# Four tiles of a gather move from ScalarE's row DMAs to GpSimd, in a graph layer on one core

## The chip, the cores and the metric

The kernel runs on one core of a Trainium2 chip. Five engines work side by side and meet at semaphores: TensorE (PE, with its weight loads PEld), VectorE (DVE), ScalarE (ACT), GpSimd (POOL) and SyncE (SP). SP, ACT and POOL each have a queue from which DMAs are issued. The metric is the device time of one execution in microseconds; lower is better. A profiled execution has its own time, and a span, which is the time from its first to its last instruction.

## The reference

A message-passing layer over 12,500 nodes of 128 features and 400,000 edges, sorted by destination, with a residual and a normalisation of rows:

```python
rbf = jnp.exp(-(distances[:, None] - centers) ** 2 / (2.0 * width * width))
cut = 0.5 * (jnp.cos(jnp.pi * distances / CUTOFF) + 1.0) * (distances <= CUTOFF)
W = (jax.nn.silu(rbf @ fw1 + fb1) @ fw2 + fb2) * cut[:, None]
messages = (h[src] @ pw + pb) * W
agg = jax.ops.segment_sum(messages, dst, num_segments=num_atoms)
y = h + (jax.nn.silu(agg @ mw1 + mb1) @ mw2 + mb2)
out = _layernorm(x + y)
```

The edge lengths are such that most edges lie beyond the cutoff and add nothing. h[src] is the gather: for every edge that counts, one row of 128 float32 (0.5 KB) from a table of nodes.

## The kernel before

**Stages.** First the table proj = x @ pw + pb is computed for all nodes, 4 x 128 rows at a time, and stored to DRAM. Beside it VectorE packs the edges: seven chunks (0 to 6) of the edge list are compacted to those within the cutoff by shifts under masks (copies under a predicate at L539, passes over the listing at L545 and L549), written to a list in DRAM by GpSimd (L524), read back and unpacked to indices, places and cutoffs. Packing goes on while the main loop runs, a few steps between one quad and the next.

**Quads.** Packed edges are taken in 139 quads (q = 0 to 138) of QT = 4 tiles of 128 edges (j = 0 to 3). For each quad: `basis` makes the radial functions on ScalarE (L1150, L1154), `first` and `silu` the first layer on TensorE and ScalarE for two quads at once (L1166, L1172), `second` the second layer into a bank of PSUM (L1184). `message` (L1200) multiplies it on VectorE with the gathered rows. `place` (L1213) makes on VectorE a 0/1 matrix, times the cutoff, of the destinations; `sum_up` (L1234) multiplies messages and matrix on TensorE into sums of a window of nodes, and `add` (L1268) adds these on VectorE to aggT. Nodes whose edges are all done go through the second network and the normalisation in between (L1282 and on). The last quad, 138, is multiplied tile by tile (L1200, four products of 128 columns).

**Who fetches the rows.** A tile's 128 rows are usually fetched by one indirect DMA of GpSimd (`fetch`, L1098) into a buffer of the quad: 13 buffers named quad and, up to quad 62, 8 more named x. The first 12 quads gather from the input x, the others from proj. In 13 quads (`SINGLY`) tile j = 0 is left out by `fetch` and comes in 128 single DMAs of one row, each with its address in a register (`one_row`, L1074), into buffers of their own (row_sb). Nine of the quads (`BY_SP`) are fetched from SP's queue, four (`BY_ACT`: 36, 68, 100, 134) from ScalarE's. ScalarE's single DMAs are put by `beside` behind its instructions in `basis` and `silu`, three, two or four at a time (`HIDE`), as long as its list of rows lasts. In such a quad `message` first waits for a semaphore that counts the rows, multiplies tile 0 alone (L1197), and then the other three tiles (L1200).

**What sets the order.** All engines' orders are written out by hand in the program; it keeps a clock of its own (`clock` for VectorE, `pool` for GpSimd, which grows by 1.29 for each gather) to decide which piece of packing to put where. A gather gets its place in two steps: `fetches` puts it on a queue when the program's clock says so, and `gathers` issues it when VectorE's program has as many instructions as the table `PACE` asks for that quad and tile (`pace` interpolates between the table's pairs of quad and count). `vectors` is the list of VectorE's instructions of some kinds, and the issued gather is tied to the one at the count: it waits on the chip until that instruction is done.

Of the kernel before, what the change touches and what calls it, by code (L numbers as in the profile page):

```python
# [57 lines left out]
DIRECT = 32  # L58
FIRST = 16
LISTS = 5  # L60
PACE = ((2, 17), (3, 26), (4, 36), (5, 54), (7, 95), (9, 125), (10, 144), (12, 170), (18, 250), (24, 324), (30, 373), (36, 458), (42, 544), (48, 612), (54, 691), (60, 754), (66, 826), (72, 902), (78, 982), (84, 1071), (90, 1139), (96, 1218), (102, 1306), (108, 1357), (114, 1414), (120, 1461), (126, 1518), (132, 1580), (138, 1646), (139, 1666))
VECTORS = ("TensorScalarPtr", "TensorTensor", "CopyPredicated", "TensorReduce", "TensorCopy",
           "BNStats")
SPILL = 4
# [6 lines left out]
PACK_US = 1.5  # L71
EARLY_US = 7
BY_SP = (22, 45, 62, 67, 86, 102, 113, 124, 135)
BY_ACT = (36, 68, 100, 134)
SINGLY = tuple(sorted(BY_SP + BY_ACT))
A_ROW = 0.58
A_ROW_LATE = 0.42
# [15 lines left out]
def kernel(  # L93
# [347 lines left out]
    vectors, queue = [], []  # L441
# [8 lines left out]
    def pace(q, j):  # L450

        (a, u), (b, v) = next((k for k in zip(PACE, PACE[1:]) if q < k[1][0]))
        return int(u + (v - u) * (q + j / QT - a) / (b - a))

    def gathers(must=0):

        while queue and (queue[0][0] < must or len(vectors) >= pace(*queue[0])):
            q, j = queue.pop(0)
            fetch(q, js=(j,))
# [372 lines left out]
    def unpack(c):  # L832
# [34 lines left out]
        def paired(dt, name):  # L867
            if c == 0:
                k = OWN_0[name]
                if k > 3:  # L870
                    return aggT[:np_, N - (k - 3) * 256:N - (k - 4) * 256].bitcast(dt)
                v = quad_sb[GOT - 1] if k < 2 else own(1, "msg", 0)
                v = v.rearrange("p j f -> p (j f)").bitcast(dt)
                return v[:np_, k % 2 * 256:k % 2 * 256 + 256]
            return work.tile([64, 256], dt, name=name, bufs=1)[:np_]
# [69 lines left out]
        if mine:  # L945
            at_row = work.tile([64, P], I32, name="at_row", bufs=3)
            nc.vector.tensor_scalar(at_row[:np_], f_src[:, :P], float(4 * H), None, op0=OP.mult)
            for q in mine:
                p = 2 * (q - QB[c])
                singles[q in BY_ACT].extend((q, e, at_row[p:p + 1]) for e in range(P))  # L950
        part = paired(I32, "part")
# [82 lines left out]
    def own(q, name, also):  # L1034

        k = q % (4 if q >= OWN_4 else 2)
        if k > 1:
            return quad_sb[OTHERS[2 * also + k - 2]]
        if (name, k) not in own_sb:
            own_sb[name, k] = keep.tile([P, QT, H], F32, name=f"{name}{k}")  # L1040
        return own_sb[name, k]
# [20 lines left out]
    def one_row(act):  # L1062

        eng, of, n = (nc.scalar, BY_ACT, ACT_AT_ONCE) if act else (nc.sync, BY_SP, AT_ONCE)
        q, e, i = singles[act].pop(0)
# [26 lines left out]
    def fetch(q, idx=None, table=None, js=range(QT)):  # L1092
        got = quad_sb[place_of(q) if q >= 0 else 0]
        for j in js:
            if q in SINGLY and j == 0:
# [4 lines left out]
                in_offset=bass.IndirectOffsetOnAxis(ap=i, axis=0))  # L1100
            if PACE[0][0] <= q < NL:
                tc.add_manual_dep(
# [85 lines left out]
    def message(q, js=(0, QT)):  # L1188
        gathers(q + 1)
        msg = own(q, "msg", 0)  # L1190
        a, b = js
        if q in SINGLY and a == 0:
            act = q in BY_ACT
            k = (BY_ACT if act else BY_SP).index(q)
            assert q in alone and all(s[0] != q for s in singles[act])
            nc.vector.wait_ge(row_sem[act][k % ROW_SEMS], 16 * P * (k // ROW_SEMS + 1))
            m = nc.vector.tensor_mul(msg[:, 0, :], pu_of[q][:, :H], alone.pop(q))  # L1197
            tc.declare_no_dep(m.ins, group="rows", reason="waits on row_sem")
            a = 1
        nc.vector.tensor_mul(msg[:, a:b, :], pu_of[q].rearrange("p (j f) -> p j f", j=QT)[:, a:b, :],  # L1200
                             got_of[q][:, a:b, :])
        if b == QT:
            free.append(pu_of.pop(q))
            got_of.pop(q)
        gathers()
        return msg
# [385 lines left out]
    for q in range(NL - 7):  # L1592
        while todo and q + 2 >= DIRECT // QT and todo[0] <= chunk_of(min(q + 2, NQ - 1)):
            go_on(todo[0])
        msg = message(q)
        nodes(q)
        most[0] = room(q)
# [71 lines left out]
    q = NL - 7  # L1669
    house(q)  # L1670
    msg = message(q)
    second(q + 2)
    sum_up(q, msg)
# [9 lines left out]
    q += 1  # L1683
    house(q)
    msg = message(q)
    second(q + 2)
    first(octs(q - 1))
# [206 lines left out]
```

## Time and profile before

| | |
|---|---|
| median of 3 runs | 715.56 us (713.54 to 716.36) |
| the profiled execution | 714.6 us, its span 713.1 us |
| mean granted TensorE clock | 0.927 |
| gathers (indirect DMAs of GpSimd into quad and x) | 48 from the input, 401 + 94 from proj |
| single-row DMAs | 1152 from SP, 512 from ScalarE, 0.5 KB each |
| moved by DMA | 91.45 MB, 128 GB/s on average |

Engines are PE, PEld, DVE, ACT, POOL and SP; an engine's name with a q (ACTq) is its sequencer, which issues DMAs and handles registers, and such instructions are not counted as busy. L1098 is line 1098 of the kernel. "out<-in" names what an instruction writes and reads. In a group, "x401" is a count, and three numbers with slashes are the shortest, median and longest duration in ns. Brackets give the idle time of the engine before an instruction and what ended it, inferred from semaphores; "issue" means that nothing in the profile was waited for. In a list of waits, "A <- B: 45.1, 21, 3.7" reads: A waited for B 45.1 us in total, 21 times, 3.7 at the longest. The chain of waits starts at the last instruction and follows back what released each step. The slices cut the span into 40 equal parts; a digit is the busy share in tenths.

### The profile page before, as it was taken

Reading aid. Unit: us, or ns where it says so; the run is one execution under the profiler, and the core shown is the slowest. Engines: PE = TensorE matmul, PEld = TensorE weight load, DVE = VectorE, ACT = ScalarE, POOL = GpSimd, SP = SyncE. Lnnn points to the kernel's source line nnn. Section 1 sums busy time; section 2 is a strip of 40 time slices with the busy share of each in tenths; the row PEclk is TensorE's granted clock in tenths of the full one; section 3 lists DMA queues with packets and bytes.
Section 4 is the critical chain, followed back from the end, with each engine's and each line's share of the span. In section 5 each row is a group of like instructions: output and inputs, shape, how many; then the busy total and the mean of one; then the engine's idle time right before and its main releaser. Section 6 shows DMA issues by size and latency. Waiting matters only on the chain.

```text
span 713.1 us, 15123 instructions
## 1 busy us (share of the span) xinstructions
PE 585.7 (82%) x3531; PEld 462.3 (65%) x3531; DVE 561.6 (79%) x1744; ACT 402.2 (56%) x568; POOL 528.5 (74%) x564
## 2 busy tenths in 40 slices
PE   6786767778988788798889997999788877798785
PEld 5775556556766576676677774777566655575673
DVE  8889899749999889989999995867554555475776
ACT  6547725144745667554665455668543843476455
POOL 6777777777777777777777777777777777777772
PEclk9999897799999899999988999999988999999998
DMA  8997443242434334342334344444442443334343
GB/s 255 338 290 227 149 127 105 61 136 84 112 102 134 85 87 116 100 131 85 98 104 116 107 136 110 142 115 142 120 123 72 128 130 97 101 102 142 92 126 105
DMA packets 54233, 91.45 MB, mean 128 GB/s; under 512 B 14384, under 2 KB 21776, under 8 KB 54138
## 3 DMA queue, kind: packets, MB, share of 16 engines
q0 software_dynamic: 17680, 36.44, 20.4%
q1 hardware_dynamic: 25172, 35.68, 15.2%
q10 hardware_dynamic: 11286, 18.31, 7.9%
q8 instruction: 29, 0.48, 0.3%
q14 instruction: 66, 0.54, 0.2%
HBM read 74.59 MB, written 15.79 MB: 127 GB/s over the span
## 4 chain that ended last, share of the span: by engine, by line
DVE 27%; DMA 15%; PE 14%; issue 8%; ACTq 4%; ACT 3%; DVEq 2%; POOL 2%; SPq 0%; POOLq 0%
DMA quad<-proj,srci 14%; DVE hot L1213 7%; PE ph L1166 4%; DVE msg L1200 4%; PE bank L1184 3%; DVE aggT L1268 3%; PE sums L1234 3%; ACTq L1074 2%; POOL quad L1098 2%; DVE quad L1213 2%; DVE bank L545 2%; DVE quad L1200 1%; DVEq L1243 1%; DVE r_d L539 1%; PE bank L1282 1%
## 5 line engine op out<-in xcount | busy, mean ns | idle before, releaser
L1098 POOL DMA_INDIRECT quad<-proj,srci x401 | 381.1, 950 | 122.4 <-issue 48.2
L1184 PEld LDWEIGHTS bank<-fw_sb,s 128*128 128x128 f32 x1112 | 160.1, 207 | 61.9 <-issue 51.6
L1184 PE MATMUL bank<-fw_sb,s 128*128 128x128 f32 x1112 | 160.5, 291 | 0.0
L1166 PE MATMUL ph<-rbf,w_sb 102*128 102x512 f32 x278 | 141.9, 635 | 13.0 <-ACT s L1172 9.5
L1234 PEld LDWEIGHTS sums<-hot,msg 128*128 128x128 f32 x816 | 108.9, 200 | 50.5 <-issue 22.8
L1172 ACT ACTIVATE s<-ph 128x1024 f32<-128x1024 f32 x70 | 71.3, 1018 | 116.9 <-PE ph L1166 116.5
L1213 DVE TENSOR_SCALAR hot<-iota_n,dl,cut 128x80 f32<-128x80 f32 (+4 forms) x408 | 109.1, 339 | 21.3 <-PE sums L1234 19.3
L1234 PE MATMUL sums<-hot,msg 128*128 128x80 f32 (+4 forms) x816 | 111.0, 281 | 12.9 <-DVE msg L1200 12.9
L1098 POOL DMA_INDIRECT x<-proj,srci x94 | 89.9, 957 | 29.2 <-issue 7.3
L1181 PE MATMUL bank<-fb_b,ones_b 96*128 96x512 bf16 x139 | 56.1, 403 | 44.2 <-DVE msg L1200 25.8
L1200 DVE TENSOR_TENSOR msg<-bank,quad 128x512 f32<-128x512 f32 (+1 forms) x78 | 52.3, 671 | 49.6 <-DMA quad<-proj,srci 45.1
L1166 PEld LDWEIGHTS ph<-rbf,w_sb 102*128 102x128 f32 x278 | 50.8, 203 | 52.4 <-issue 37.3
L1268 DVE TENSOR_TENSOR aggT<-aggT,sums 128x80 f32 (+4 forms) x209 | 53.9, 258 | 21.1 <-PE sums L1234 7.2
L1150 ACT ACTIVATE rbf<-d_sb,rbf_bias,rbf_scale 102x512 f32<-102x512 f32 x70 | 56.2, 803 | 7.8 <-issue 7.8
L1098 POOL DMA_INDIRECT quad<-in_x_dram,srci x48 | 47.5, 989 | 16.3 <-issue 5.5
L1172 ACT ACT_TABLE_LOAD x35 | 44.9, 1283 | 15.3 <-issue 14.9
L1154 ACT ACT_TABLE_LOAD x35 | 44.9, 1283 | 11.3 <-issue 9.4
L349 PEld LDWEIGHTS bank<-pw_sb,xT 128*128 128x128 f32 (+1 forms) x292 | 41.6, 207 | 13.3 <-ACT xT L1005 7.2
L1154 ACT ACTIVATE rbf<-rbf 102x512 f32<-102x512 f32 x70 | 44.1, 630 | 8.1 <-issue 5.7
L1234 PE MATMUL sums<-quad,quad 128*128 128x128 f32 (+3 forms) x296 | 42.8, 290 | 4.7 <-DVE quad L1200 4.6
L1200 DVE TENSOR_TENSOR quad<-bank,quad 128x512 f32<-128x512 f32 (+2 forms) x40 | 25.1, 628 | 26.9 <-DMA quad<-proj,srci 26.7
L1234 PEld LDWEIGHTS sums<-quad,quad 128*128 128x128 f32 x296 | 39.6, 206 | 6.9 <-DVE quad L1200 6.2
(281 smaller groups left out, 813.4 us busy)
## 6 DMA issues: line engine op xcount, KB each, us to landing
row_sb<-proj SPq DMA_DIRECT2D x1152, 0.5 KB
d_sb<-near_d ACTq DMA_DIRECT2D x67, 256.0 KB
x<-in_x_dram SPq DMA_DIRECT2D x46, 256.0 KB
row_sb<-proj ACTq DMA_DIRECT2D x512, 0.5 KB
quad<-proj,srci POOLq DMA_INDIRECT x401
proj<-hp SPq DMA_DIRECT2D x24, 256.0 KB
out_dram<-x SPq DMA_DIRECT2D x22, 256.0 KB
x<-proj,srci POOLq DMA_INDIRECT x94
```

Source lines behind the costliest of these rows:

```text
L349: nc.tensor.matmul(to[:m, k, :], lT[:, k * P:k * P + m], w, start=False, stop=(k == a + c - 1))
L1098: g = nc.gpsimd.indirect_dma_start(out=got[:, j, :], out_offset=None, in_=proj if table is None else table, in_offset=bass.IndirectOffsetO ...
L1150: a = nc.scalar.activation(rbf[:u], d[:u], AF.Square, bias=rbf_bias[:u], scale=rbf_scale[:u])
L1154: nc.scalar.activation(rbf[:u], rbf[:u], AF.Exp, scale=-1.0 / (2.0 * width * width))
L1166: nc.tensor.matmul(ph[:, h, :], w1_sb[:2 * KR, h, :], rbf[:2 * KR], start=True, stop=True)
L1172: nc.scalar.activation(s[:, :n], ph[:, :n], AF.Silu)
L1181: nc.tensor.matmul(pu, ones_b[:, :P], bias_b["fb2"].rearrange("k j f -> k (j f)"), start=True, stop=False)
L1184: nc.tensor.matmul(pu[:, j * H:(j + 1) * H], s[:, j * P:(j + 1) * P], fw2_sb, start=False, stop=(j == QT - 1))
L1200: nc.vector.tensor_mul(msg[:, a:b, :], pu_of[q].rearrange("p (j f) -> p j f", j=QT)[:, a:b, :], got_of[q][:, a:b, :])
L1213: nc.vector.tensor_scalar(hot[:, j, :wide(q)], iota_n[:, :wide(q)], dl[:, at[0], at[1]], cut[:, at[0], at[1]], op0=OP.is_equal, op1=OP.mult)
L1234: nc.tensor.matmul(pa[:, k * W:k * W + wide(q)], msg[:, j, :], hot[:, j, :wide(q)], start=(j % n == 0), stop=(j % n == n - 1))
L1268: nc.vector.tensor_add(to, to, pa[:, k * W:k * W + wide(q)])
```

## The change

ScalarE's list of quads becomes empty: tile 0 of quads 36, 68, 100 and 134 is gathered by GpSimd like any other tile, and these quads are multiplied in one product. SP keeps its nine. In the quads of SP, the product of tile 0 is taken off the list `vectors` at once, so that gathers are neither tied to it nor counted with it, and the counts in `PACE` are lower by as many from quad 42 on.

```diff
-PACE = ((2, 17), (3, 26), (4, 36), (5, 54), (7, 95), (9, 125), (10, 144), (12, 170), (18, 250), (24, 324), (30, 373), (36, 458), (42, 544), (48, 612), (54, 691), (60, 754), (66, 826), (72, 902), (78, 982), (84, 1071), (90, 1139), (96, 1218), (102, 1306), (108, 1357), (114, 1414), (120, 1461), (126, 1518), (132, 1580), (138, 1646), (139, 1666))
+PACE = ((2, 17), (3, 26), (4, 36), (5, 54), (7, 95), (9, 125), (10, 144), (12, 170), (18, 250), (24, 324), (30, 373), (36, 458), (42, 543), (48, 611), (54, 688), (60, 751), (66, 823), (72, 898), (78, 978), (84, 1065), (90, 1133), (96, 1211), (102, 1298), (108, 1349), (114, 1404), (120, 1452), (126, 1507), (132, 1569), (138, 1635), (139, 1653))
...
-BY_ACT = (36, 68, 100, 134)
+BY_ACT = ()
...
             m = nc.vector.tensor_mul(msg[:, 0, :], pu_of[q][:, :H], alone.pop(q))
+            vectors.pop()
             tc.declare_no_dep(m.ins, group="rows", reason="waits on row_sem")
```

## The prediction

> **What bounds the kernel now.** I began with the page's busy shares and slices, to see which engine never lets go:
>
> ```profile
> span 713.1 us, 15123 instructions
> ...
> PE 585.7 (82%) x3531; PEld 462.3 (65%) x3531; DVE 561.6 (79%) x1744; ACT 402.2 (56%) x568; POOL 528.5 (74%) x564
> ...
> DVE  8889899749999889989999995867554555475776
> ...
> POOL 6777777777777777777777777777777777777772
> ```
>
> By shares, PE leads and GpSimd is fourth. The slices say otherwise: VectorE is at nine tenths up to two thirds of the span and then falls to five, while GpSimd stands at seven in all slices but the first and last. An engine that is at one constant level below ten either gets its work at a constant rate, or has a constant gap after each instruction. The groups by line and the instructions in order of time decide (start, duration, engine, line, operation, in brackets the idle time before and what ended it):
>
> ```profile
> L1098 POOL DMA_INDIRECT quad<-proj,srci x401: 938/944/1188, 72.5 to 700.3; - x134
> L1098 POOL DMA_INDIRECT x<-proj,srci x94: 940/944/1097, 77.6 to 327.2; - x94
> ...
> L524 POOL DMA_INDIRECT packed<-line,at_i x7 | 7.3, 1043 | 2.7 <-issue 1.2 <-DVE base_i L661 0.9 <-DVE hot L1213 0.3
> ```
>
> ```profile
> 194.30 0.94 POOL L1098 DMA_INDIRECT x<-proj,srci  x1 [0.30 <-issue]
> 195.54 0.94 POOL L1098 DMA_INDIRECT x<-proj,srci  x1 [0.30 <-issue]
> ...
> 208.48 1.01 POOL L1098 DMA_INDIRECT x<-proj,srci  x1 [0.75 <-DVE hot L1213]
> ...
> 212.33 1.01 POOL L1098 DMA_INDIRECT x<-proj,srci  x1 [0.34 <-DVE hot L1213]
> ...
> 254.29 0.94 POOL L1098 DMA_INDIRECT quad<-proj,srci  x1 [0.39 <-DVE bank L545]
> ...
> 699.02 0.94 POOL L1098 DMA_INDIRECT quad<-proj,srci  x1 [0.30 <-issue]
> 700.27 0.94 POOL L1098 DMA_INDIRECT quad<-proj,srci  x1 [0.30 <-issue]
> ```
>
> A gather takes 0.944 us and the next starts 0.30 us later whatever is named as the releaser: a step of 1.25 us. From 72.5 to 700.3, 627.8 us, lie 401 + 94 = 495 gathers, which at 1.25 fill 618.8; the list writes in between (1.04 + 0.30 each, at most 7) take up to 9.4 more. The stream is full for 627.8 of 713.1 us. Only three gaps after 72.5 are over 0.31: 0.75, 0.34 and 0.39, together 0.45 + 0.04 + 0.09 = 0.6 us of real waiting, all for VectorE.
>
> The last question is whether the end hangs on the last gather. VectorE's products of the last quad:
>
> ```profile
> 699.98 0.27 DVE L1200 TENSOR_TENSOR quad<-bank,quad 128x128 f32<-128x128 f32 x1
> ...
> 701.13 0.28 DVE L1200 TENSOR_TENSOR quad<-bank,quad 128x128 f32<-128x128 f32 x1
> ...
> 702.43 0.28 DVE L1200 TENSOR_TENSOR quad<-bank,quad 128x128 f32<-128x128 f32 x1
> ...
> 703.29 0.29 DVE L1200 TENSOR_TENSOR quad<-bank,quad 128x128 f32<-128x128 f32 x1
> ```
>
> The quad is multiplied tile by tile as its four gathers land; the second and third products follow the gathers' step (1.15, 1.30 us), and the last starts 3.0 us after the last gather's start. So the end is that start plus 12.8 us (713.1 - 700.27). The kernel is a stream of gathers on one engine with a fixed tail.
>
> **The change, part by part.** First, what is taken from ScalarE:
>
> ```profile
> L1074 ACTq MOVE row_sb<-proj x512: 29/29/38, 145.3 to 640.6; - x171
> L1074 ACTq DMA_DIRECT2D row_sb<-proj x512: 227/228/543, 145.4 to 640.7; - x171
> L1197 DVE TENSOR_TENSOR msg<-bank,row_sb x8: 271/281/285, 202.4 to 635.2; 128x128 f32<-128x128 f32 x8
> L1197 DVE TENSOR_TENSOR quad<-bank,row_sb x5: 266/283/290, 375.0 to 690.1; 128x128 f32<-128x128 f32 x5
> ```
>
> 512 x (0.029 + 0.228) = 131.6 us of ScalarE's queue go, with the loads of the row addresses. That work sits in waits ScalarE has anyway, but not all of it:
>
> ```profile
> by line: DMA quad<-proj,srci 13.9%; issue 7.7%; DVE hot L1213 6.5%; PE ph L1166 4.5%; DVE msg L1200 3.8%; PE bank L1184 3.3%; DVE aggT L1268 2.8%; PE sums L1234 2.6%; ACTq L1074 2.3%; POOL quad L1098 1.8%; DVE quad L1213 1.8%; DVE bank L545
> ...
> ACT s L1172 <- PE ph L1166: 116.5, 46, 6.9
> ...
> DVE msg L1200 <- DMA quad<-proj,srci: 45.1, 21, 3.7
> ...
> DVE quad L1200 <- DMA quad<-proj,srci: 26.7, 15, 3.0
> ```
>
> The chain of waits puts 2.3%, 16.4 us, on ScalarE's row issues. I book this at nothing: the chain follows one path back, and beside it GpSimd went on without a gap. What ScalarE gains, PE and VectorE get earlier, and spend waiting for gathers, as VectorE already does for 45.1 + 26.7 us. Were GpSimd's stream not full, up to 16.4 us would come out (second rival).
>
> Second, VectorE. Of the 13 extra products of 0.28 us, four go; their quads' other product grows from 384 to 512 columns:
>
> ```profile
> 632.39 0.69 DVE L1200 TENSOR_TENSOR quad<-bank,quad 128x512 f32<-128x512 f32 x1 [2.88 <-DMA quad<-proj,srci]
> ...
> 635.76 0.56 DVE L1200 TENSOR_TENSOR msg<-bank,quad 128x384 f32<-128x384 f32 x1 [0.29 <-DMA quad<-proj,srci]
> ```
>
> That is 4 x (0.28 + 0.56 - 0.69) = 0.6 us less work, hidden in the same waits; the bound of cost is 0 to -0.6 us. These quads now wait for one more gather in place of a semaphore of rows; nothing else is queued behind that wait than before.
>
> Third, GpSimd gets four gathers of 128 rows, one each for quads 36, 68, 100 and 134, each just before its quad's other three. All later gathers, and the list writes after quad 36, are queued behind them. The bytes (512 rows of 0.5 KB) are the same and only change queues. A stretch without packing and one with VectorE nearly full give the same price (length, then busy time and count of PE, PEld, DVE, ACT, POOL, then clock, DMA share, GB/s):
>
> ```profile
> 200.00:320.00 120.00, 102.67 (x630) 82.02 (x629) 108.92 (x313) 72.49 (x88) 90.44 (x96) 0.93 0.37 106
> ...
> 480.00:701.00 221.00, 183.94 (x1080) 140.05 (x1078) 134.14 (x468) 127.81 (x187) 167.19 (x177) 0.95 0.40 113
> ```
>
> 120 / 96 = 1.25 and 221 / 177 = 1.249. Four make **+5.0 us**. Bounds: by the shortest, 4 x (0.938 + 0.30) = 4.95; by the longest, 4 x (1.188 + 0.30) = 5.95; I take the step, which most have.
>
> What lengthens a gather speaks on whether it is cheaper with ScalarE silent. The longest:
>
> ```profile
> 372.97 1.19 POOL L1098 DMA_INDIRECT quad<-proj,srci  x1 [0.31 <-DMA quad<-proj,srci]
> ...
> L1098 POOL DMA_INDIRECT quad<-proj,srci x401 | 381.1, 950 | 122.4 <-issue 48.2 <-DVE hot L1213 11.6 <-DVE aggT L1268 11.6
> L1098 POOL DMA_INDIRECT x<-proj,srci x94 | 89.9, 957 | 29.2 <-issue 7.3 <-DVE hot L1213 4.4 <-DMA x<-proj,srci 3.0
> ```
>
> Means of 950 and 957 against a median of 944 leave 401 x 6 + 94 x 13 = 3.6 us of lengthening in all; that is what could at most vanish. I take 0 of it: in 480 to 701, where ScalarE still issues rows, the mean is 167.19 / 177 = 0.945, so the rows lengthen nothing.
>
> The Trainium skill's page "SBUF — State Buffer", section "SBUF: two separate sides", has a rule against this change: a DMA that GpSimd issues needs descriptors written through a port pair that some VectorE instructions lock, while one issued by ScalarE does not. Its section "A bandwidth-pool intuition that's wrong (but worth ruling out)" gives 620 ns alone and some 3,100 ns beside a VectorE copy; by that factor of five, an estimate, four gathers would cost about 20 us. This trace shows nothing of that size, 1.19 us being its worst after 72.5.
>
> Fourth, the ties. A gather waits for a VectorE instruction that is counted in the list of names. The nine remaining row products leave the list and four cease to exist; the table's last entry falls by 13 (1666 to 1653), entries before quad 36 stay. So each gather stays tied to the same place in VectorE's work, give or take one instruction (0.3 us). As GpSimd comes 1.25 us later to each tie after quad 36, the three waits of 0.6 us in all should shrink. VectorE may be later too, since the program's own clock for GpSimd gains 1.29 us per added gather and may pull packing steps ahead (one listing pass: 0.69 us). Bounds -0.6 to +0.7; I take -0.4, the two late ones being short and the 0.75 being smaller than one added step.
>
> Sum: 5.0 - 0.4 = +4.6 us on a span of 713.1: 717.7. The profiled run took 714.6, 1.5 more than its span, and so 719.2; it lies 1.0 under the median of 715.56, so the median to expect is **720.2 us**, +0.64%.
>
> **Rivals.**
>
> 1. *The gathers get shorter (no change).* If rows and gathers do contend and all 3.6 us of lengthening and the 0.6 of waits go: 5.0 - 4.2 = +0.8, 716.4. For it: row fetches and gathers share the DMA engines. Against: the mean of 0.945 above.
> 2. *ScalarE's queue was the path (faster).* Its place is the stretch 145 to 641; the price is the 16.4 us of the chain, against 5.0 of gathers: 715.56 - 11.4 = 704.2. It decides as soon as GpSimd has idle time that VectorE or ScalarE causes; from 3.6 us of such time on, the result leaves "no change". The waits of 0.75 to 0.34 between 208 and 255 speak for it, their sum of 0.6 against it.
> 3. *The ties catch.* If VectorE's order shifts so that packing stands ahead of tied instructions where GpSimd is close behind (208 to 255), each of the two additions within the packing, quads 36 and 68, costs another 1.3 us: 5.0 + 2.6 = +7.6, 723.2. For it: the 0.39 behind a listing pass. Against: GpSimd is later too.
> 4. *Gathers starve beside VectorE.* If the freed ScalarE packs VectorE's work closer, so that all gathers after quad 36 (103 quads, some 400) come at the 957 ns of those into x, which run up to 327 us where VectorE is fullest, and not at 945: 400 x 0.012 = 4.8 on top of 4.6, 725.0. Against: VectorE's total work falls. It is the Trainium skill's rule above ("SBUF — State Buffer", "SBUF: two separate sides") at the size that the rows give.
>
> That the change does not do what it says can be ruled out from the code: with no quad for ScalarE, its list stays empty and the gathers are no longer skipped.
>
> **How the numbers follow.** Forecast 0.75, rivals 0.10, 0.05, 0.07, 0.03. The range is 717.8 (the sum less the shortened gathers' first 2 us and a low median) to 723.0 (the longest gathers and the tie's 0.7, or nearly all of rival 3). A measurement of this kernel tells about 0.5%, 3.6 us, from no change. Faster: rival 2, 0.05. Same: rival 1, and 0.04 from the forecast's low edge, 0.14. Slower: 0.81.
>
> **What would show it.** Gathers in the changed profile: 404 + 95 (quad 36 lands in an x buffer), step still 1.25; the last gather's start at about 705 in place of 700.27, and 12.8 us from there to the end; no row DMA on ScalarE's queue; ScalarE's row issue gone from the chain and the share of gathers in it higher. VectorE's waits for gathers after 480 should not fall below today's. It is wrong if gaps over 0.31 on GpSimd add up to several us (rival 3), if the mean gather falls to 0.944 everywhere (rival 1), or if the last gather starts before 704 (rival 2).

## The result, and the profile after

The changed kernel takes 720.03 us (median of 14, 717.29 to 723.71), the kernel before 716.09 us (median of 14, 713.54 to 719.91): ratio 1.0044, 95% interval 1.0025 to 1.0063. A second comparison (e8 below) gave 719.55 against 715.2 us: 1.0061, interval 1.0044 to 1.0079. Forecast were 720.2 us and +4.6 us; measured are +3.9 and +4.4. That the median of 720.03 lies within 0.2 us of the forecast is in part luck: the kernel before came out 0.5 us above the 715.56 from which the forecast was reckoned, and the difference 0.7 us under the forecast one. One thing has to be known for what follows: ten of the twelve experiments met chips in a condition in which the kernel before itself takes 982 to 999 us in place of 715, so their ratios are read only among themselves.

The page of the changed kernel:

```profile
span 718.7 us, 14062 instructions
...
PE 589.0 (82%) x3531; PEld 462.4 (64%) x3531; DVE 561.5 (78%) x1740; ACT 399.2 (56%) x568; POOL 531.7 (74%) x568
...
POOL 6777777777777777777777777777777777777771
...
L1098 POOL DMA_INDIRECT quad<-proj,srci x404 | 383.4, 949 | 123.2 <-issue 44.5
...
L1172 ACT ACTIVATE s<-ph 128x1024 f32<-128x1024 f32 x70 | 71.2, 1018 | 182.7 <-PE ph L1166 182.6
...
L1098 POOL DMA_INDIRECT x<-proj,srci x95 | 91.0, 958 | 29.0 <-issue 7.3
...
L1172 ACT ACT_TABLE_LOAD x35 | 44.9, 1283 | 0.8 <-issue 0.2
L1154 ACT ACT_TABLE_LOAD x35 | 44.9, 1283 | 0.6
```

ScalarE's table loads in the page of before:

```profile
L1172 ACT ACT_TABLE_LOAD x35 | 44.9, 1283 | 15.3 <-issue 14.9
L1154 ACT ACT_TABLE_LOAD x35 | 44.9, 1283 | 11.3 <-issue 9.4
```

GpSimd's slices are the same flat sevens. Its gathers are 404 + 95 = 499, four more, of the same 0.95 us. The idle time before ScalarE's table loads has gone with the row issues, and its wait for PE at L1172 has grown from 116.5 to 182.6 us: ScalarE spends what it was given on waiting.

The gathers' end and the products of the last quad, in order of time:

```profile
702.53 0.95 POOL L1098 DMA_INDIRECT quad<-proj,srci  x1 [0.30 <-issue]
703.78 0.94 POOL L1098 DMA_INDIRECT quad<-proj,srci  x1 [0.30 <-issue]
```

```profile
703.95 0.28 DVE L1201 TENSOR_TENSOR quad<-bank,quad 128x128 f32<-128x128 f32 x1
...
705.41 0.29 DVE L1201 TENSOR_TENSOR quad<-bank,quad 128x128 f32<-128x128 f32 x1
...
708.22 0.29 DVE L1201 TENSOR_TENSOR quad<-bank,quad 128x128 f32<-128x128 f32 x1 [2.00 <-DMA quad<-proj,srci]
```

The last gather starts at 703.78 in place of 700.27: +3.5 us. From there to the end of the span are 14.9 us, not 12.8: +2.1. The two make the 5.6 us by which this profiled span is longer. Most of the 2.1 lies in the last landing: from the gather's start to the product that waits for it are 4.44 us, where before they were 3.02. While it is waited for, PE has nothing to do, and its granted clock falls (PE's next matmul; then stretches with length, PE's busy time and count, granted clock, DMA share, GB/s):

```profile
708.56 0.80 PE L1235 MATMUL sums<-quad,quad 128*128 128x128 f32 x2 [1.76 <-DVE quad L1201]
```

```profile
706.00:707.00 1.00, 0.80 (x7) 1.00 0.10 18
707.00:708.00 1.00, 0.00 (x0) 1.00 0.37 137
708.00:709.00 1.00, 0.44 (x2) 0.69 1.02 352
709.00:711.00 2.00, 1.79 (x6) 0.50 0.09 29
```

In the kernel before the clock falls too (0.63 from 708 to 710 us), but there PE's last matmul has ended by then, at 706.3.

VectorE's waits for gathers are about the same in total, 45.8 + 26.6 against 45.1 + 26.7:

```profile
DVE msg L1201 <- DMA quad<-proj,srci: 45.8, 21, 4.1
...
DVE quad L1201 <- DMA quad<-proj,srci: 26.6, 14, 3.6
```

### The profile page after: what moved, and what is told of

It is laid out like the page before. It is cut to its first block, busy times and chain, and to the rows that moved or that the text cites. A ratio compares the mean times of both kernels' runs of the same rounds, so it can differ in the third digit from the quotient of the medians.

```text
span 718.7 us, 14062 instructions
## 1 busy us (share of the span) xinstructions
PE 589.0 (82%) x3531; PEld 462.4 (64%) x3531; DVE 561.5 (78%) x1740; ACT 399.2 (56%) x568; POOL 531.7 (74%) x568
## 5 line engine op out<-in xcount | busy, mean ns | idle before, releaser
L1172 ACT ACTIVATE s<-ph 128x1024 f32<-128x1024 f32 x70 | 71.2, 1018 | 182.7 <-PE ph L1166 182.6
L1235 PEld LDWEIGHTS sums<-hot,msg 128*128 128x128 f32 x816 | 107.1, 197 | 48.3 <-issue 24.0
L1201 DVE TENSOR_TENSOR msg<-bank,quad 128x512 f32<-128x512 f32 (+1 forms) x78 | 52.7, 675 | 50.2 <-DMA quad<-proj,srci 45.8
L1235 PE MATMUL sums<-quad,quad 128*128 128x128 f32 (+3 forms) x296 | 44.9, 299 | 14.0 <-DVE quad L1201 14.0
L1201 DVE TENSOR_TENSOR quad<-bank,quad 128x512 f32<-128x512 f32 (+2 forms) x40 | 25.3, 632 | 34.6 <-DMA quad<-proj,srci 26.6
L1235 PEld LDWEIGHTS sums<-quad,quad 128*128 128x128 f32 x296 | 41.5, 214 | 16.5 <-DVE quad L1201 15.9
```

The source lines that it names most:

```text
L1172: nc.scalar.activation(s[:, :n], ph[:, :n], AF.Silu)
L1235: nc.tensor.matmul(pa[:, k * W:k * W + wide(q)], msg[:, j, :], hot[:, j, :wide(q)], start=(j % n == 0), stop=(j % n == n - 1))
```

## The experiments

### Where the kernel before takes 715 us: more gathers (e8, e9)

e8 is the change itself. e9 goes on in the same direction: SP's nine tiles are gathered too, and no row DMA is left.

```diff
-BY_SP = (22, 45, 62, 67, 86, 102, 113, 124, 135)
+BY_SP = ()
```

> The changed kernel itself, beside the kernel before on this chip. If the chip runs the kernel before in some 716 us: 1.0044 to 1.0064. If in some 980 to 1000 us, where row DMAs are dear: sum of e2 (four gathers more, rows kept: 1.0055) and of e3 and e5 (512 rows less: 0.985), so 0.990 (0.985 to 0.997).

> The changed kernel with SP's nine tiles gathered by GpSimd too: no row DMA is left, 563 indirect DMAs, 13 more than before. With the stream full (716 us before): 13 x 1.25 = 16.3 us less 1 us, ratio 1.021 (1.018 to 1.024). With gaps in the stream (1000 us before): faster than e4's 0.951, 0.92 to 0.95, since the other 640 row DMAs go as well. Rival there (not the rows, but the place of e4's four quads made it faster): 0.95 to 0.96 again.

Measured, beside the same runs of the kernel before (715.2 us): e8 719.55 us, 1.0061 (1.0044 to 1.0079); e9 736.75 us, 1.0296 (1.0265 to 1.0327). e8 gives the change again, 4.4 us for four gathers, inside what was expected. e9 is beyond what was expected (1.018 to 1.024): 21.6 us, where 13 gathers make 16.3. Its page and its gathers and products in order of time:

```profile
span 736.5 us, 11718 instructions
```

```profile
592.68 0.94 POOL L1098 DMA_INDIRECT quad<-proj,srci  x1 [1.78 <-DVE msg L1201]
...
596.42 0.94 POOL L1098 DMA_INDIRECT quad<-proj,srci  x1 [1.55 <-DVE msg L1201]
...
638.25 0.94 POOL L1098 DMA_INDIRECT quad<-proj,srci  x1 [1.43 <-DVE msg L1201]
...
721.64 0.94 POOL L1098 DMA_INDIRECT quad<-proj,srci  x1 [0.30 <-issue]
```

```profile
DVE msg L1201 <- DMA quad<-proj,srci: 61.9, 29, 5.6
...
DVE quad L1201 <- DMA quad<-proj,srci: 50.7, 26, 6.0
```

The last gather starts at 721.64, 21.4 us later than before: 16.3 for the gathers, and 5.4 for what eight gaps have over 0.30 us, less the waits that are gone. GpSimd now stands still up to 1.78 us for VectorE's products, and VectorE waits 112.6 us in all for gathers (72 before): each of the two waits for the other in turn. The gather at 592.68 shows how: counted in order it fetches the last tile of quad 113, and it is held by the product of quad 112 at 591.72, which itself had waited 4.55 us for its own gathers. That product reads another quad's buffer, so it is the tie that holds the gather. All gaps over 0.32 us lie behind 554 us. Up to 480 us the gathers come at the rate of before, here in e9 and then in the kernel before (length, busy time and count of gathers, clock, DMA share, GB/s):

```profile
72.00:200.00 128.00, 94.81 (x101) 0.83 0.38 109
200.00:320.00 120.00, 90.06 (x95) 0.97 0.37 105
320.00:480.00 160.00, 119.31 (x126) 0.93 0.40 112
```

```profile
72.00:200.00 128.00, 94.88 (x101) 0.87 0.38 112
200.00:320.00 120.00, 89.45 (x95) 0.93 0.37 106
320.00:480.00 160.00, 119.45 (x125) 0.94 0.40 113
```

322 in 408 us; before there were 101 + 95 + 125 = 321. With tiles added among them and no more gathers per time, every later quad comes later by its full step: VectorE at nine tenths in the packing half hides none of it. The ties catch with thirteen gathers, of which four show nothing. But it isn't the third rival as it was forecast: that one has packing ahead of tied instructions between 208 and 255 us, and here the gaps lie behind the packing (its last pass at L545 starts at 410.8 in e9), where the tied products wait for gathers themselves.

| kernel | gathers and list writes | last gather's start | from there to its product | span |
|---|---|---|---|---|
| before | 550 | 700.27 | 3.02 | 713.1 |
| changed | 554 | 703.78 | 4.44 | 718.7 |
| e8, the same | 554 | 704.21 | 3.86 | 717.6 |
| e9 | 563 | 721.64 | 4.08 | 736.5 |

### Where the kernel before takes 982 to 999 us (e1 to e7, e10 to e12)

Three sets of runs, on three chips, met this condition. One of those chips ran e8 and e9 at 715 us later, so it does not belong to the chip for good. What it is can be seen in the kernel with the ties alone (e1), which issues the same DMAs as the kernel before. The page, then the row issues:

```profile
span 998.8 us, 15122 instructions
...
PE 665.2 (67%) x3531; PEld 518.8 (52%) x3531; DVE 566.1 (57%) x1744; ACT 403.7 (40%) x568; POOL 529.6 (53%) x564
...
POOL 6345546565655565665645655555665165416540
...
PE 22%; issue 20%; SPq 19%; DVE 12%; another core or an unknown queue 10%; ACT 4%; ACTq 3%; DMA 2%; POOL 2%; DVEq 1%; POOLq 0%
SPq L1074 16%; PE ph L1166 5%; PE sums L1235 5%; PE bank L1184 4%; DVE hot L1214 3%; PE bank L349 3%; ACTq L1074 2%; SPq L1070 2%; DVE msg L1201 2%; PE bank L1181 1%; POOL x L1098 1%; SPq L192 1%; DVE aggT L1269 1%; DVE bank L545 1%
...
L1098 POOL DMA_INDIRECT quad<-proj,srci x401 | 382.8, 955 | 321.7 <-issue 98.2
```

```profile
L1074 SPq MOVE row_sb<-proj x1152: 2/29/1451, 119.4 to 974.3; - x192
L1074 SPq DMA_DIRECT2D row_sb<-proj x1152: 2/228/1406, 119.5 to 974.4; - x192
```

```profile
DVE msg L1197 <- DMA row_sb<-proj: 44.2, 2, 26.9
...
DVE quad L1197 <- DMA row_sb<-proj: 8.5, 1, 8.5
```

VectorE, ScalarE and GpSimd are busy as long as ever to within 1% (GpSimd 529.6 us, a gather 0.955), and PE longer at a mean granted clock of 0.797 against 0.927; but there are pauses between instructions: 321.7 us of idle time before the quad gathers where there were 122.4. A MOVE of SP's queue, 29 ns in the median and 38 at most before, takes up to 1451. SP's row issues hold 16% of the chain, more than any other line of the kernel, and products of tiles by rows wait for rows (44.2 + 8.5 us), which none did in the profile of before. Counted in order, the three that wait are those of quads 113, 124 and 135, all fetched by SP. The chain is a weaker witness here: 10% of it, and 93.4 us of ScalarE's waits at L1172 alone, are put down to a releaser that the profile does not know, and the profile of before has no such wait. The transfers themselves took no longer: the packets of GpSimd's queue fill 14.3% of 998.8 us, 143 us, and 20.4% of 713.1, 145 us, before. What causes the pauses isn't shown by the profile and stays open. What the experiments say of it is the price of a row there.

**Ties alone (e1).** The kernel before, with the line `vectors.pop()` and the changed `PACE`.

> The kernel before with the second half of the change alone: the 13 products of tiles by rows leave the list of VectorE's instructions and the changed table of counts is used; ScalarE still fetches its four tiles. Theory of the gather stream (the span is the number of gathers times 1.25 us plus a tail): 550 indirect DMAs as before, gaps over 0.30 within 0.6 us of before, ratio to before 1.000 within 0.002. Rival (the ties cost or save something by themselves): gaps on GpSimd move by more than 1 us and the ratio leaves 0.998 to 1.002.

997.67 against 999.19 us, 0.9992 (0.995 to 1.0035): no effect that can be told, but the interval is 4 to 5 us to either side, and the gaps of this condition make its profile useless for the point on gaps of 0.6 us.

**Gathers added, rows kept (e2, e11).** The changed kernel, in which ScalarE goes on issuing its rows and VectorE waits for their semaphore, but multiplies the gathered tile:

```diff
+IDLE = (36, 68, 100, 134)
...
-            singles[q in BY_ACT].extend((q, e, at_row[p:p + 1]) for e in range(P))
+            singles[q in IDLE].extend((q, e, at_row[p:p + 1]) for e in range(P))
...
+        if q in IDLE and a == 0:
+            alone.pop(q)
+            nc.vector.wait_ge(row_sem[1][IDLE.index(q) % ROW_SEMS], 16 * P * (IDLE.index(q) // ROW_SEMS + 1))
```

> The changed kernel, with ScalarE still issuing its 512 row DMAs into buffers that no product reads (VectorE still waits for their semaphore); GpSimd gathers the four tiles as in the changed kernel. Theory of the gather stream: 554 indirect DMAs, no change from the changed kernel, 1.0044 (within 0.0025) of before. Rival (ScalarE's freed 131.6 us of queue time gave back part of the 5.0 us): slower than the changed kernel, 1.0064 and above. Rival (rows lengthen gathers): sum of gather time over 0.944 us rises by more than 1 us against the changed kernel's 2.6.

> The kernel of e2 once more (the changed kernel, and ScalarE still issues 512 row DMAs that no product reads), for a chip that runs the kernel before in some 716 us. Gather stream: 554 indirect DMAs, the changed kernel's ratio, 1.0061 (1.004 to 1.008). Rival (ScalarE's freed queue gave something back): the difference between this and the changed kernel on this chip, 1.0061, is over 0.002.

1.0055 (1.0009 to 1.010) and 1.0081 (1.004 to 1.0122): 5 to 8 us, about the four gathers' price or somewhat more, though the stream is full of gaps.

**Rows taken away, no gathers added (e3, e5, e10).** In the kernel before, ScalarE's list stays empty, and in its four quads

```diff
-            m = nc.vector.tensor_mul(msg[:, 0, :], pu_of[q][:, :H], alone.pop(q))
+            if act:
+                nc.vector.tensor_mul(msg[:, 0, :], pu_of[q][:, :H], got_of[q][:, 1, :])
```

> The kernel before, with ScalarE's four tiles fetched by nobody: the product of tile 0 of quads 36, 68, 100 and 134 reads the rows of tile 1 in their place, so 512 rows are left out of the computation. ScalarE's queue is as free as in the changed kernel, GpSimd's stream as short as before. Theory of the gather stream: 550 indirect DMAs, ratio to before 0.9985 (the waits of 0.6 us and some lengthening at most), not under 0.997. Rival (ScalarE's row issues were on the path, 16.4 us by the chain of waits): 0.977 to 0.993.

> The same kernel as e3: ScalarE's four tiles fetched by nobody, tile 0 of quads 36, 68, 100 and 134 multiplied with the rows of tile 1, 512 rows left out. If this chip runs the kernel before in some 716 us with GpSimd's gathers back to back: gather stream 0.9985 (0.997 to 1.000); rival (ScalarE's row issues on the path) 0.977 to 0.993. If the chip runs the kernel before in some 1000 us with gaps of 250 us in the stream, the ratio of e3, 0.985, should come again.

> The kernel of e3 and e5 once more (ScalarE's four tiles fetched by nobody, tile 0 of four quads multiplied with the rows of tile 1, 512 rows left out), for a chip that runs the kernel before in some 716 us. Gather stream: 550 indirect DMAs without gaps, ratio 0.9985 (0.997 to 1.000). Rival (ScalarE's row issues were on the path, 16.4 us by the chain of waits): 0.977 to 0.993.

0.9845 (0.9793 to 0.9897), 0.9856 (0.9812 to 0.9901), 0.982 (0.9765 to 0.9875): 14 to 18 us less for 512 rows. In this condition the rows have a price of the size that the second rival gave them. That ScalarE's queue is the path is not shown by it: in e1 no product waits for a row of ScalarE's. In e3's profile the same three products wait for SP's rows, 9.7 + 18.7 + 8.3 us where e1 has 17.3 + 26.9 + 8.5, so that a part of the gain is SP's rows coming less late; by which way, stays open. On a chip at 715 us this was not measured.

**Eight gathers more, 1024 rows fewer (e4, e6).** The changed kernel with `BY_SP = (22, 62, 86, 113, 135)`.

> The changed kernel with four of SP's nine tiles (quads 45, 67, 102, 124) gathered by GpSimd too: 558 indirect DMAs, eight more than before. Theory of the gather stream: 8 x 1.25 = 10.0 us less some 1 us that waits and lengthening give back, ratio 1.0125 (1.010 to 1.015), the last gather's start at about 709. Rival (only some of the four gathers cost, since VectorE bounds the packing half up to 430 us): the two in that half, quads 45 and 67, add nothing, and the ratio stays under 1.010.

> The same kernel as e4: eight gathers more than before, four from ScalarE and four from SP. With the stream full (716 us before): ratio 1.0125 (1.010 to 1.015), last gather's start at about 709; rival (the gathers of the packing half, quads 36, 45, 67 and 68, add nothing, since VectorE bounds that half) 1.005 to 1.008. With the stream full of gaps (1000 us before): 0.95 as in e4, since 1024 row DMAs less are to be issued.

0.9512 (0.946 to 0.9565) and 0.9536 (0.9487 to 0.9585): 46 to 49 us faster. The page of e6, first line, and the groups by line:

```profile
span 928.2 us, 13026 instructions
```

```profile
L1098 POOL DMA_INDIRECT quad<-proj,srci x408 | 387.1, 949 | 271.3 <-issue 88.9 <-DVE aggT L1269 57.7 <-DVE hot L1214 47.1
```

Seven more quad gathers than in e1 (which ran on another chip) and 50 us less idle time before them, and in e6's chain of waits SP's queue no longer appears. What the edit takes away is row issues, so they are what was saved; by e5, on the chip of e6, ScalarE's 512 make up some 14 us of it, and the rest would be SP's. e4's expectation was made for a full stream, and nothing of it could be tested here.

**Three gathers fewer, 384 rows more (e7, e12).** The ties of the changed kernel, with

```diff
-BY_SP = (22, 45, 62, 67, 86, 102, 113, 124, 135)
-BY_ACT = (36, 68, 100, 134)
+BY_SP = (22, 45, 62, 67, 86, 102, 110, 117, 124, 131, 136)
+BY_ACT = (36, 68, 100, 118, 134)
...
-A_ROW_LATE = 0.42
+A_ROW_LATE = 0.29
...
-HIDE = (3, 2, 4)
+HIDE = (5, 4, 6)
```

> The ties of the changed kernel, with ScalarE keeping its four tiles and taking a fifth (quad 118), and SP taking eleven (22, 45, 62, 67, 86, 102, 110, 117, 124, 131, 136), its rows issued closer together after the packing: 547 indirect DMAs, three fewer than before, and 384 more row DMAs. Gather stream: -3.75 us, ratio 0.9948 (0.993 to 0.997) where the stream is full. Rival (row DMAs have a price of their own, in queues or contention, that eats what a gather saves): 0.998 or above. On a chip where the kernel before takes 1000 us: slower, 1.01 to 1.04, by the 384 rows.

> The kernel of e7 once more (three gathers fewer than before, 384 row DMAs more, after quad 100 closer together), for a chip that runs the kernel before in some 716 us. Gather stream: 547 indirect DMAs, -3.75 us, ratio 0.9948 (0.993 to 0.997). Rival (row DMAs closer together arrive late, and products of tiles by rows wait for them): waits of the products at L1198 for row_sb in the profile, ratio 0.998 or above. A chip in the state of e1 to e7 tells nothing new, 0.985, 1.0055 and 1.11.

1.1105 (1.1055 to 1.1155) and 1.1115 (1.1057 to 1.1173): 110 us slower, far beyond the 1.04 that was thought possible. Who waited for rows in e12:

```profile
DVE msg L1198 <- DMA row_sb<-proj: 98.3, 3, 37.3
...
DVE quad L1198 <- DMA row_sb<-proj: 35.1, 2, 24.9
```

133 us of VectorE's time goes into five waits for rows. Counted in order they are those of quads 110, 117, 124, 131 and 136, all of them SP's: in this condition SP does not issue them at the pace asked for. Whether this version beats both kernels on a chip at 715 us, as the stream's price of -3.75 us says, was not measured.

## Why the prediction was right

**GpSimd's stream as the bound: right.** Four gathers added, the same step, no idle time, and an end that moved by about their sum; e9 puts nine more on it and moves the end by at least their sum. That the stream was full was the whole argument, and the runs at 982 to 999 us are a counter-test of a kind: there the stream has hundreds of us of gaps, and a kernel with more gathers and fewer rows is the faster one (e4, e6).

**The price of a gather, 1.25 us each, 5.0 in all: right.** The added gather of quad 36 stands in the changed stream like any other:

```profile
193.99 0.94 POOL L1098 DMA_INDIRECT x<-proj,srci  x1 [0.30 <-DMA packed<-line,at_i]
195.24 0.94 POOL L1098 DMA_INDIRECT x<-proj,srci  x1 [0.30 <-DVE bank L545]
```

**What comes back, -0.4: a little small.** The three waits of 0.6 us in all have gone (no gap over 0.32 after 72.5 us), so that -0.6 was right and not -0.4. The lengthening, booked at 0, fell from 3.6 to 404 x 5 + 95 x 14 = 3.35 us, and the first gather starts 0.2 us earlier (6.70 for 6.87). That gives 5.0 - 0.6 - 0.3 - 0.2 = +3.9 for the last gather's start, measured +3.5, and +3.9 in e8. Rival 1 has a grain of truth, but of 0.3 us and not 3.6.

**The fixed tail of 12.8 us: the step that was mis-sized.** It took 14.9 in the changed profile, and 13.4 in e8 (717.6 - 704.21). The last landing is not a constant: 3.0 us in the one profile of before, 3.9 to 4.4 in three profiles of longer streams. The two errors, 0.7 to 1.1 us too much on the stream and 0.6 to 2.1 too little on the tail, have opposite signs. Whether the longer landing comes with the change or varies from run to run was not tried (SP issues the last seven stores of results from 0.5 us before the last gather on in the kernel before, and from 1.1, 1.7 and 1.9 us before it in the changed one, e8 and e9, but the landing does not grow in that order: 4.44, 3.86, 4.08); the runs of one kernel alone spread over 6 us.

**ScalarE at nothing: right where the stream is full, as far as can be seen.** More was taken off its queue than the 131.6 us, since 32 loads of row addresses at L1070 went too, 1.3 us each, 41.5 in all. Yet ScalarE is idle for 319.5 us (718.7 - 399.2) where it was idle for 310.9 (713.1 - 402.2), and 66 us more of that time end with PE (182.6 - 116.5). The chain's 16.4 us did not come out: with them, the kernel would have become faster. This is shown by the profile and by the sum, which leave room for some tenths of a us; the experiments with the rows alone (e2, e3) all fell into the other condition, where 512 rows cost 14 to 18 us.

**VectorE's 0.6 us and the ties: right, as far as seen.** VectorE's work is 561.5 against 561.6 us. The ties had no effect that can be told in e1, which is in the other condition, and with four gathers none held GpSimd up; with thirteen they did (e9), and there a gather cost 21.6 / 13 = 1.66 us on average.

**The signs set beforehand: three did not come.** The last gather starts at 703.78, and a start before 704 was to mean that ScalarE's queue had been the path. But GpSimd has no gap over 0.32 us left, e8's last gather starts at 704.21, and the sum above gives +3.9 with nothing from ScalarE: the line was drawn too close to the forecast of 705. VectorE's waits for gathers after 480 us were not to fall, and are 66.8 us against 68.7 before (62.3 in e8); why stays open. And the chain of waits of the changed profile reaches back over little more than 1% of the span, so the shares of row issues and gathers in it cannot be compared.

**The rule on the locked port.** By the Trainium skill's page "SBUF — State Buffer", section "SBUF: two separate sides", VectorE could have starved the added gathers. The means of 949 and 958 ns, against 950 and 957 before, show nothing of it. Which of this kernel's VectorE instructions would take the lock, no run here shows.

## What to carry to other kernels

An engine at a flat seven tenths from the first slice to the last can be the one that is full: look at the step between its instructions, not at its busy share, and multiply. Once this stream was full, work taken off another engine was worth nothing that could be seen, however much of the chain of waits it held; and the price read from the stream held only until the ties made GpSimd and its consumer wait for each other (1.25 us for each of four, 1.66 on average for thirteen). An edit of the same kind can have the other sign in another condition of the chip (e4, e6), so look at the kernel before in the same runs before reading a ratio.

## What the runs showed of the hardware that was not expected

The same kernel took 715 and 982 us on one chip at different times. VectorE, ScalarE and GpSimd worked as long in both; the difference lies in pauses between instructions, where a MOVE of 29 ns on SP's queue took up to 1451, and in PE's lower granted clock (0.797). A tile fetched row by row costs 128 x 0.26 = 33 us of a queue, besides the loads of its addresses, and where the kernel takes 715 us that is hidden; in the other condition, 512 rows cost 14 to 18 us of the kernel's time. And in the tail, PE's 1.76 us without work were enough for its granted clock to fall to 0.69 and then 0.50.
